# Router logits from 32x32 squares of x turned by VectorE, in a gated cross-attention kernel

## The chip, the cores and the metric

The kernel runs on one core of one Trainium2 chip, in f32. The metric is the device time of one execution in microseconds. Times before are the median of three runs; one further execution was profiled.

## The reference

For a batch of 8, x is 512 x 2048 (features by positions) per batch. Two blocks follow each other: attention within windows of 128 positions, then a router over 64 experts whose tokens are the 512 feature rows.

```python
x = x + jnp.tanh(g_xattn[0]) * xattn(_layernorm(x), ctx, masks, ...)   # D=512, 8 heads of 32, windows of 128
x = x + jnp.tanh(g_ffn[0]) * ffn(_layernorm(x), router_weight, router_bias, expert_bias)

# xattn: q = Wq xn + bq; k = Wk xn + bk; v = Wv ctx + bv        (Wq, Wk, Wv: 256 x 512)
#        attn = softmax(q.T k / sqrt(32), masked); o = gelu(attn v)
#        out = (Wo o + bo) * masks
# ffn:   logits = flat @ router_weight.T + router_bias           (flat: tokens x 2048, 64 experts)
#        w_dense = top-8 of softmax(logits), zero elsewhere; w_sum = their sum
#        out = flat * w_sum + w_dense @ expert_bias
```

The logits sum over the 2048 positions. On the chip x lies with its 512 rows on partitions and the positions along the free axis, so the logits need x turned: positions on the partitions.

## The kernel before

Work is cut into chunks of 512 positions, four per batch, 32 in all, and each chunk into two steps `g`, an even and an odd one, of 256 positions (two windows). Each engine works through its own queue in the order in which the program is written out by hand (`manual_schedule`); SyncE (SP) issues nearly all DMAs from one queue. PSUM has eight banks: `ps_sc` has four (`sc0` to `sc3`, one buffer each), `ps_tr` two (tag `tr`), `ps_mm` two (tag `mm`, taken in turn by `product`).

One step does, in this order:

- `scores(g)`: 16 products for q.T k in 32x128 tiles into the four score banks. `maxima` on VectorE adds the mask and takes row minima, `exps` on ScalarE follows group by group (four groups of four), `divide` is a reciprocal on VectorE and a multiplication on POOL for each half.
- `attend(ch, m)`: the output projection `po` of a finished chunk, 128 rows at a time. VectorE evicts it into `t` (L561), POOL adds it to x in `xr` (L564). Rows 0 and 1 are done in the odd step, in banks `sc1` and `sc2` once the last stage (`steps`) runs, rows 2 and 3 in the next even step, in `mm` banks.
- `queries_and_keys(nxt, e, between)`: q and k of the next chunk, by a scheme of seven block products instead of eight (L356) with sums on VectorE and POOL (L363 to L381). Other work of the step is called from inside it through `between(0)` and `between(1)`.
- `turn_blocks` (L492): VectorE turns the attention weights in 32x32 squares, in two instructions; `move_blocks` (L504): 16 DMAs from SP bring the squares to their places. `weigh` (L523) uses them one step later.
- `values` (L391): v of the next windows, copied out by ScalarE.
- `read_x`: two pieces of a later batch's x (`raw`) get their statistics on VectorE (L251), and SP is told to load the next two.
- `sums_of_x` on POOL and `norm` on ScalarE prepare the chunk after the next.

The second block runs behind. `turn_x(ch, k)` turns one 128-position piece of a finished chunk of x by four TensorE transposes into a `tr` bank (`px`, L579), and ScalarE copies it to `x1T`; there are four such pieces per chunk, all in an even step. `logits(ch)` (L590) in the next odd step multiplies them by the router weights in 64-column halves, right after `exps(g, 1)`; `logits_out` (L606, L608) adds the result to `lgT`. `statistics2` (L574) takes the second layernorm's statistics. When a batch's four chunks are in, the experts are chosen (`gather_halves`, `choose`, `select`, `keep_selected`), and in the eight steps after that `scale_x` on POOL and `mix` (`mixed` L739, `added` L757) finish one eighth of the batch each and store it.

Of the kernel before, what the change touches and what calls it, by code (L numbers as in the profile page):

```python
# [9 lines left out]
F32 = mybir.dt.float32  # L10
# [5 lines left out]
P = 128  # L16
# [6 lines left out]
def flamingo_gated_kernel(  # L23
# [49 lines left out]
    small = ctx.enter_context(tc.tile_pool(name="small", bufs=2))  # L73
    ps_sc = ctx.enter_context(tc.tile_pool(name="ps_sc", bufs=1, space=PSUM))
# [48 lines left out]
    rw_sb = const.tile([P, NK, E], F32, name="rw_sb")  # L123
    eb_sb = const.tile([2 * E, S], F32, name="eb_sb")
# [49 lines left out]
    def load_experts():  # L174
        for i in range(2):
            nc.sync.dma_start(eb_sb[i * E : (i + 1) * E, :], eb)
# [121 lines left out]
    def mask(ch):  # L298

        biases[ch] = work.tile([P, CW], F32, tag="bias", name=f"bias_{ch}")  # L300
        nc.vector.tensor_scalar(biases[ch], mks[ch], 0.0, NEG, ALU.is_le, ALU.mult)
# [39 lines left out]
    def queries_and_keys(ch, e, between):  # L341
# [21 lines left out]
        nc.vector.tensor_copy(s1, p1)  # L363
        nc.vector.tensor_tensor(u2, p6, s1, ALU.add)  # L364
        banks.append(product([P, 2, CW // 2], f"qk_{ch}_{e}_1"))
# [3 lines left out]
        nc.vector.tensor_copy(s5, p5)  # L369
        nc.gpsimd.tensor_tensor(u4, u2, s5, ALU.add)  # L370
        between(0)
        banks.append(product([P, 2, CW // 2], f"qk_{ch}_{e}_2"))
# [5 lines left out]
        between(1)  # L378
        banks.append(product([P, 2, CW // 2], f"qk_{ch}_{e}_3"))
        p4 = block(6, w22, t_[:, 2, :, :])  # L380
        nc.vector.tensor_tensor(q[:, c1], p4, u3, ALU.add)  # L381

    pvs = {}

    def values(ch, h, i, r=None):

        if (ch, h) not in pvs:
            pvs[ch, h] = product([P, NPP, DK], f"pv_{ch}_{h}", r)
# [153 lines left out]
    x1T, lgT, pos, pls = {}, {}, {}, {}  # L542
# [8 lines left out]
    def attend(ch, m, cs=whole, r=None, engine=None, tag=("x1T", 4)):  # L551
# [24 lines left out]
    def turn_x(ch, k, engine=nc.scalar):  # L576
        px = ps_tr.tile([P, NM, P], F32, tag="tr", name=f"px_{ch}_{k}")
        for m in range(NM):
            nc.tensor.transpose(px[:, m, :], xr[ch][:, m, k * P : (k + 1) * P], ident)  # L579
        t = work.tile([P, NM, P], F32, tag="x1T", name=f"x1T_{ch}_{k}", bufs=4)  # L580
        copy(engine, t, px)
        x1T[ch, k] = t

    def logits(ch, ms=slice(0, NM)):


        pl = product([P, D], f"pl_{ch}_{ms.start}")
        for k in range(KC):
            rows = slice((k % 2) * E, (k % 2 + 1) * E)
            nc.tensor.matmul(  # L590
                pl[rows, ms.start * P : ms.stop * P], rw_sb[:, (ch % NCH) * KC + k, :],
                x1T[ch, k][:, ms, :].rearrange("p m d -> p (m d)"),
                start=(k < 2), stop=(k >= KC - 2),
            )
        if ms.stop == NM:
            for k in range(KC):
                del x1T[ch, k]
        pls[ch] = pl

    def logits_out(ch, ms=slice(0, NM)):  # L600
        b = ch // NCH
        ds = slice(ms.start * P, ms.stop * P)
        pl = pls.pop(ch)[:, ds]
        if ch % NCH == 0:
            lgT[b] = work.tile([P, D], F32, tag="lgT", name=f"lgT_{b}", bufs=1)
            nc.vector.tensor_copy(lgT[b], pl)  # L606
        else:
            nc.vector.tensor_tensor(lgT[b][:, ds], pl, lgT[b][:, ds], ALU.add)  # L608
# [123 lines left out]
    def mixed(b, k, stop=True):  # L732
# [3 lines left out]
        for i in range(2):  # L736
# [3 lines left out]
                pt, experts[b]["wT"][rows, mp, :], eb_sb[rows, j * CW : (j + 1) * CW],  # L740
# [111 lines left out]
    for g in range(NG - NH):  # L852
# [20 lines left out]
        def turn_x_(k):  # L873
            if xch is not None:
                turn_x(xch, k)


# [6 lines left out]

        scores(g)
        maxima(g, (0, 1))
# [8 lines left out]

        exps(g, 0)
        exps(g, 1)
        if even and xch is not None:
            attend(xch, 2)
        if lch is not None:  # L900
            logits(lch)
            logits_out(lch)
        maxima(g, (2, 3))
        if even:
            if xch is not None:
# [4 lines left out]
        exps(g, 2)  # L910
# [331 lines left out]
```

## Time and profile before

| | before |
|---|---|
| median of 3 runs | 1237.62 us (1237.52 to 1242.6) |
| profiled execution, its own time | 1242.64 us |
| its span | 1240.9 us |
| granted TensorE clock, mean | 0.996 |
| busy: TensorE, VectorE, ScalarE, POOL | 97%, 78%, 64%, 64% |
| DMA, all queues | 236 MB, mean 190 GB/s |

A row of a group in the profile reads: line, engine, operation, output from input, shapes, count, then busy time in us, the mean of one in ns, and the idle time just before these instructions with what ended it. PE is TensorE, DVE VectorE, ACT ScalarE, SPq the DMA issuing queue of SyncE. A step lasts about 18.3 us, so a chunk about 36.6. Durations of one instruction overlap the next one's start on VectorE and ScalarE, so occupancy is read from start to start.

### The profile page before, as it was taken

To read this page: it belongs to the slowest core of one execution; us is meant where nothing else is said; L and a number is where in the kernel's file an instruction comes from. 1 tells how busy PE (TensorE), PEld (TensorE's weight loads), DVE (VectorE), ACT (ScalarE), POOL (GpSimd) and SP (SyncE) were. 2 spreads that over 40 slices of the span, in tenths; PEclk is the share of its full clock that TensorE was granted. 3 is DMA by queue.
4 is the path that set the end of the run, shared out by engine and by line. 5 is a ranking of instruction groups with operands and counts; after the bars stand their busy time and mean duration, and the time that the engine had idled before them with its cause. 6 is when DMAs were issued, how large, how long until landed. Compare 5 with 4: busy or idle time off the path is not lost.

```text
span 1240.9 us, 27273 instructions
## 1 busy us (share of the span) xinstructions
PE 1209.3 (97%) x8572; PEld 840.5 (68%) x8572; DVE 968.7 (78%) x3549; ACT 795.8 (64%) x2717; POOL 792.5 (64%) x817
## 2 busy tenths in 40 slices
PE   8899989999999999999999999999999999999997
PEld 5766767777677677676677667667667667667553
DVE  5677757888778878888878887788877887778776
ACT  2766646767566657657657566667656757656663
POOL 3654655666577665678566677565667666578544
PEclk9999989999999999999999999999999999999999
DMA  8346655666776676676776676676676766565434
GB/s 288 91 133 178 167 166 134 188 194 190 209 232 196 196 223 185 204 225 183 219 224 190 195 228 198 199 221 182 204 230 199 210 188 193 152 196 160 137 121 184
DMA packets 157280, 236.22 MB, mean 190 GB/s; under 512 B 26192, under 2 KB 60496, under 8 KB 157008
## 3 DMA queue, kind: packets, MB, share of 16 engines
q1 hardware_dynamic: 154816, 231.60, 63.5%
q10 hardware_dynamic: 2320, 2.88, 0.7%
q8 instruction: 68, 1.11, 0.4%
q14 instruction: 76, 0.62, 0.2%
HBM read 137.93 MB, written 33.55 MB: 138 GB/s over the span
## 4 chain that ended last, share of the span: by engine, by line
PE 79%; DVE 8%; DMA 5%; ACT 3%; POOL 2%; issue 2%; SPq 1%; DVEq 0%; ACTq 0%; POOLq 0%
PE qk L356 25%; PE po L555 16%; PE pv L391 16%; PE pa L523 5%; PE sc L419 5%; PE pb L739 4%; PE px L579 4%; PE pl L590 3%; DVE at L442 3%; ACT at L454 2%; DMA raw<-in_x 2%; DMA xr<-in_x 1%; SPq L504 1%; DMA mk<-in_mask_Bx1x_ff 1%; DVE st L251 1%
## 5 line engine op out<-in xcount | busy, mean ns | idle before, releaser
L454 ACT ACTIVATE at<-at,nmx 128x128 f32<-128x128 f32 x1024 | 395.1, 388 | 211.6 <-DVE nmx L442 198.2
L463 POOL TENSOR_TENSOR at<-at,rsum 128x1024 f32<-128x1024 f32 x128 | 242.6, 1895 | 263.1 <-DVE rsum L462 263.1
L391 PE MATMUL pv<-wv_sb,cx 128*128 128x256 f32 x1024 | 250.2, 388 | 2.1 <-DMA cx<-in_ctx 2.1
L555 PE MATMUL po<-o,wo_sb 128*128 128x512 f32 x512 | 234.0, 599 | 0.0
L442 DVE CUSTOM_DVE_ANT_0 at<-sc,bias 128x128 f32<-128x128 f32 x1024 | 224.8, 285 | 10.1 <-PE sc L419 10.1
L564 POOL TENSOR_TENSOR xr<-t,xr 128x512 f32<-128x512 f32 x124 | 156.2, 1272 | 101.2 <-DVE t L561 101.0
L391 PEld LDWEIGHTS pv<-wv_sb,cx 128*128 128x128 f32 x1024 | 187.9, 191 | 38.3 <-issue 12.1
L454 ACT ACTIVATION_READ_ACCUMULATOR at<-at,nmx 128x1 f32 x1024 | 191.8, 187 | 0.0
L492 DVE STREAM_TRANSPOSE blocks<-at 128x1024 f32<-128x1024 f32 x120 | 148.0, 1234 | 23.0 <-DMA atT<-blocks 13.3
L555 PEld LDWEIGHTS po<-o,wo_sb 128*128 128x128 f32 x512 | 94.5, 190 | 97.8 <-issue 83.0
L356 PE MATMUL qk<-xt,wq_sb 128*128 128x256 f32 x496 | 128.7, 382 | 6.7 <-DVE qs L364 6.7
L397 ACT COPY x1T<-px 128x512 f32<-128x512 f32 x120 | 69.0, 583 | 99.2 <-PE px L579 98.1
L356 PE MATMUL qk<-xn,wk_sb 128*128 128x256 f32 x496 | 131.4, 387 | 0.5 <-DVE lgT L606 0.3
L356 PE MATMUL qk<-xn,ws 128*128 128x256 f32 x496 | 127.3, 379 | 0.0
L356 PEld LDWEIGHTS qk<-xn,wk_sb 128*128 128x128 f32 x496 | 89.0, 189 | 51.5 <-DVE nmx L442 29.4
L561 DVE SCALAR_TENSOR_TENSOR t<-po,bo_sb,mk 128x512 f32<-128x512 f32 x128 | 94.8, 746 | 34.8 <-PE po L555 34.5
L356 PEld LDWEIGHTS qk<-xt,wq_sb 128*128 128x128 f32 x496 | 89.3, 190 | 22.4 <-DVE qs L364 10.1
L757 DVE TENSOR_TENSOR xr<-pb,xr 128x512 f32<-128x512 f32 x122 | 78.1, 684 | 33.1 <-PE pb L739 32.5
L356 PEld LDWEIGHTS qk<-xn,ws 128*128 128x128 f32 x496 | 94.2, 190 | 12.8
L251 DVE BATCH_NORM_STATS2 st<-raw 128x6 f32<-128x512 f32 x112 | 72.3, 677 | 34.7 <-DMA raw<-in_x 34.4
L419 PEld LDWEIGHTS sc<-ks,qs 32*128 32x128 f32 x2048 | 65.0, 186 | 47.7 <-issue 22.9
L728 POOL TENSOR_SCALAR xr<-xr,xa,xd 128x512 f32<-128x512 f32 x120 | 92.5, 780 | 0.9
(123 smaller groups left out, 1845.6 us busy)
## 6 DMA issues: line engine op xcount, KB each, us to landing
atT<-blocks SPq DMA_DIRECT2D x960, 64.0 KB, 2.5
out_dram<-xr SPq DMA_DIRECT2D x63, 512.0 KB, 5.9
cx<-in_ctx SPq DMA_DIRECT2D x61, 512.0 KB, 7.6
raw<-in_x SPq DMA_DIRECT2D x112, 256.0 KB, 4.9
xn<-in_x SPq DMA_DIRECT2D x112, 256.0 KB, 3.6
xr<-in_x SPq DMA_DIRECT2D x28, 1024.0 KB, 6.1
mk<-in_mask_Bx1x_ff SPq DMA_DIRECT2D x32, 256.0 KB, 7.2
xr<-in_x SPq DMA_DIRECT2D x12, 256.0 KB, 6.7
```

What stands on the lines that cost most here:

```text
L251: nc.vector.bn_stats(st1[b][:, m, piece, :], x_)
L356: nc.tensor.matmul(out_, w_[:, j, es], xb[:, j, :], start=(j == 0), stop=(j == NM // 2 - 1))
L391: nc.tensor.matmul(pv[:, i, :], cx[:, m, i * W : (i + 1) * W], wv_sb[:, m, :], start=(m == 0), stop=(m == NM - 1),)
L419: nc.tensor.matmul(sc[r][:, i, e, :], qss[ch][rows[r], e, ws], kss[ch][rows[r], e, ws], start=True, stop=True,)
L442: nc.vector.tensor_tensor_reduce(p["at"][i][:, e * HR + r, :], p["sc"][r][:, i, e, :], bias, -scale, BIG, ALU.add, ALU.min, p["nmx"][:, r, ...
L454: nc.scalar.activation(at, at, AF.Exp, bias=p["nmx"][:, r, i, e : e + 1], scale=-1.0, accum_out=p["rsum"][:, i, h : h + 1],)
L463: (engine or nc.gpsimd).tensor_tensor(p["at"][i], p["at"][i], rs[:, :, None].to_broadcast([P, H, W]), ALU.mult)
L492: nc.vector.transpose(p["blocks"][:, :, i, :, :].rearrange("p b h j -> p h b j"), p["at"][i].rearrange("p h (b j) -> p h b j", j=Q),)
L555: nc.tensor.matmul(po[:, cs], wo_sb[:, e, m * P : (m + 1) * P], os_[ch][:, e, cs], start=(e == 0), stop=(e == NE - 1),)
L561: nc.vector.scalar_tensor_tensor(t[:, cs], po[:, cs], bo_sb[:, m : m + 1], mks[ch][:, cs], ALU.add, ALU.mult)
L564: (engine or nc.gpsimd).tensor_tensor(xc, t[:, cs], xc, ALU.add)
L728: nc.gpsimd.tensor_scalar(xc, xc, a, d, ALU.mult, ALU.add)
```

## The change

The logits no longer use x turned by TensorE. VectorE turns x in squares of 32x32 (`turn_x(ch, ms)`, one instruction of 128x512 for each 128 rows), two in the even and two in the odd step, each followed by `statistics2`. A square keeps its 32 rows' partition strip, so `logits` becomes 64 products of 32 positions by 64 experts by 128 rows in 32x64 tiles, into the four score banks, and the router weights are needed in each strip. They are spread once through DRAM (`spread_router`) and loaded for each chunk (`load_router`, 512 KB, from SP in even steps). To make room, the expert biases are loaded again in quarters (`load_experts(j)`), the mask bias has one buffer, and `t` three.

The order changes as well. `queries_and_keys` becomes a generator: its first two pairs of blocks now stand between the exps, its third bank is a `tr` one, and two of its copies go from VectorE to ScalarE. `logits` moves from behind `exps(g, 1)` to behind the first half of `values`, which takes a `tr` bank in odd steps. Choosing the experts moves accordingly.

```diff
-    def load_experts():
+    def load_experts(j):
+        t = work.tile([2 * E, CW], F32, tag="eb", name="eb")
         for i in range(2):
-            nc.sync.dma_start(eb_sb[i * E : (i + 1) * E, :], eb)
+            nc.sync.dma_start(t[i * E : (i + 1) * E, :], eb[:, j * CW : (j + 1) * CW])
+        ebs[j] = t
...
+    def load_router(ch, tag="rw"):
+        t = work.tile([P, NQ, KC, E], F32, tag=tag, name=f"rw_{ch}", bufs=1)
+        nc.sync.dma_start(
+            t.rearrange("p a k e -> p (a k e)"),
+            rw_four[ch % NCH, :, :, :].rearrange("r s f -> (r s) f"),
+        )
+        rws[ch] = t
...
-    def queries_and_keys(ch, e, between):
+    def queries_and_keys(ch, e):
...
-        nc.vector.tensor_copy(s1, p1)
+        nc.scalar.copy(s1, p1)
         nc.vector.tensor_tensor(u2, p6, s1, ALU.add)
+        yield
...
-        nc.vector.tensor_copy(s5, p5)
+        nc.scalar.copy(s5, p5)
         nc.gpsimd.tensor_tensor(u4, u2, s5, ALU.add)
-        between(0)
-        banks.append(product([P, 2, CW // 2], f"qk_{ch}_{e}_2"))
+        yield
+        banks.append(ps_tr.tile([P, 2, CW // 2], F32, tag="tr", name=f"qk_{ch}_{e}_2"))
...
-    def turn_x(ch, k, engine=nc.scalar):
-        px = ps_tr.tile([P, NM, P], F32, tag="tr", name=f"px_{ch}_{k}")
-        for m in range(NM):
-            nc.tensor.transpose(px[:, m, :], xr[ch][:, m, k * P : (k + 1) * P], ident)
-        t = work.tile([P, NM, P], F32, tag="x1T", name=f"x1T_{ch}_{k}", bufs=4)
-        copy(engine, t, px)
-        x1T[ch, k] = t
+    def turn_x(ch, ms, tag="x1b"):
...
+        for m in ms:
+            nc.vector.transpose(
+                x1b[ch][:, :, m, :], xr[ch][:, m, :].rearrange("p (b j) -> p b j", j=Q)
+            )
...
-        pl = product([P, D], f"pl_{ch}_{ms.start}")
-        for k in range(KC):
-            rows = slice((k % 2) * E, (k % 2 + 1) * E)
...
+            pl = [
+                ps_sc.tile([P, n, Q], F32, tag=f"sc{a}", name=f"pl_{ch}_{a}") for a in range(NQ)
+            ]
+        for s_ in range(NB):
+            half_ = slice((s_ % 2) * E, (s_ % 2 + 1) * E)
+            for a in range(NQ):
+                rows = slice(a * Q, (a + 1) * Q)
+                nc.tensor.matmul(
+                    pl[a][half_, :, :].rearrange("p m d -> p (m d)"),
+                    rws[ch][rows, s_ % NQ, s_ // NQ, :],
+                    x1b[ch][rows, s_, ms, :].rearrange("p m d -> p (m d)"),
+                    start=(s_ < 2), stop=(s_ >= NB - 2),
+                )
...
+        for a, pt in enumerate(pls.pop(ch)):
+            t = whole_[:, ms, a, :]
...
+                nc.vector.tensor_tensor(t, pt, t, ALU.add)
...
+        if steps and mk % 2 == 0:
+            load_experts(mk // 2)
+
         scores(g)
-        maxima(g, (0, 1))
+        maxima(g, (0, 1) if even else (0, 1, 2))
...
+        products = queries_and_keys(nxt, h)
         exps(g, 0)
...
+            next(products)
+            exps(g, 2)
+            next(products)
+        else:
+            next(products)
+            maxima(g, (3,))
+            exps(g, 1)
+            next(products)
+            exps(g, 2)
         exps(g, 3)
...
+                if ch >= 2:
+                    ms = (0, 1) if even else (2, 3)
+                    turn_x(ch - 2, ms)
+                    for m in ms:
+                        statistics2(ch - 2, m)
...
-        queries_and_keys(nxt, h, between)
+        between(0)
+        next(products)
+        between(1)
...
+        if xch is not None:
+            load_router(xch)
...
+        if g == 1 or g > 4:
+            read_x(PER)
...
-                values(c_, h_, 0, 0 if g > 1 else None)
+                values(c_, h_, 0, "tr" if g > 1 else None)
+            if lch is not None:
+                logits(lch)
+                logits_out(lch)
             weigh_between()
```

In the new odd step VectorE's queue therefore reads: maxima, evictions of the first two block pairs, the mask, the second reciprocal, `turn_x`, `statistics2`, evictions of the last blocks, `turn_blocks` twice, `read_x`, `logits_out`, the evictions of `po`, the additions of `mix`.

## The prediction

> **What bounds the kernel now.** First the page's busy shares and its chain by engine:
>
> ```profile
> PE 1209.3 (97%) x8572; PEld 840.5 (68%) x8572; DVE 968.7 (78%) x3549; ACT 795.8 (64%) x2717; POOL 792.5 (64%) x817
> ...
> PE 79%; DVE 8%; DMA 5%; ACT 3%; POOL 2%; issue 2%; SPq 1%; DVEq 0%; ACTq 0%; POOLq 0%
> ```
>
> PE is the bound, nearly without holes. Next the chain in order of time, for one even step (from 612.5 us) and the start of the odd one; each row is start, us, matmuls:
>
> ```profile
> 612.58 1.10 PE sc L419 x32
> 613.69 3.63 PE po L555 x8
> 617.32 5.20 PE qk L356 x24
> 622.51 0.44 PE px L579 x4
> ...
> 626.42 1.01 PE pa L523 x32
> ...
> 631.95 1.87 PE pl L590 x8
> 633.82 6.24 PE qk L356 x28
> ```
>
> The next even step's scores start at 649.14 in the timeline, so a pair of steps (one chunk) takes 36.63 us. Every f32 product shows as two records. Then VectorE and the DMA queue of SyncE in that pair, since the change puts work on both:
>
> ```profile
> 625.53 1.23 DVE L492 STREAM_TRANSPOSE blocks<-at 128x1024 f32<-128x1024 f32 x1
> 626.69 2.43 DVE L574 BATCH_NORM_STATS2 st<-xr 128x6 f32<-128x512 f32 x4
> ...
> 645.51 1.39 DVE L251 BATCH_NORM_STATS2 st<-raw 128x6 f32<-128x512 f32 x2 [2.13 <-DMA raw<-in_x]
> ```
>
> ```profile
> 626.80 11.32 SPq L504 DMA_DIRECT2D atT<-blocks  x16
> 638.16 0.58 SPq L115 DMA_DIRECT2D xr<-in_x  x1
> 638.84 0.95 SPq L92 DMA_DIRECT2D raw<-in_x  x2
> ```
>
> See how they hang together: the 16 block moves start when VectorE's second block transpose ends (626.8), take SP 11.32 us, and the raw loads queue behind them. So the odd step's statistics wait for a load that lands 6.7 us after its issue at 638.84. Today that wait of 2.13 us hurts nobody, because PE needs nothing from VectorE until `po`'s evictions.
>
> **PE's saving.** Per chunk, 16 transposes go (0.44 us per four: 1.75) and the old `pl` (1.87): 3.62. What comes is 64 products in 32x64 tiles, 128 records of 128 columns. No row shows that tile. Bounds: `pa` runs 32 such records on four tiles in 1.01 us; if eight tiles go no faster, 128 take 4.05; if eight overlap as four do, 2.0. I take 2.0: `pl`'s two column halves already overlap fully (8 records of 512 columns in 1.87 against 3.63 for `po`'s 8) and `sc`'s four row groups nearly so (1.10). Net 1.6 us per chunk, 31 chunks: 50 us, while PE stays the bound. At the other end, 4.05, PE loses 0.4 per chunk.
> [...]
>
> **The other engines per pair.** VectorE loses four 256-wide copies (24.5+25.7 us over 31 pairs: 1.6), gains four transposes of 128x512 (half of 1.16 start to start is 0.58, the row itself 0.7 with a fixed part; I take 0.63: 2.5) and four logits additions for one (between a quarter of 0.69 and the 256-wide 0.42; I take 0.25: +0.3): net +1.2. At 78% it has room on average. ScalarE trades four 128x512 copies (583 ns) for four of 256 (between the 352 ns of a 128-wide one and 583; 0.35 of occupancy). SP gains three issues, some 1.5 us. The single bias buffer and three `t` buffers cost nothing: VectorE rewrites the mask after its own maxima, and POOL's adds (1.27 each) end long before the third next `attend`; without that cover, one add per pair. On averages all fits; the question is the order.
>
> **Where the order puts it: the even step.** Zero is its first score. Engines work through their queues in order; the trace shows that order as written. PE: scores to 1.1, two `po` to 4.65, first qk pair to 6.4, second to 8.1; results are seen 0.17 later (6.54, 8.28). ScalarE starts the exps at 1.76, one each 0.385: eight are done at 4.85. Now it has a copy of `p1` in its queue, and behind it the rest of the exps: it waits to 6.57, copies to 6.9, four exps to 8.45, copies `p5` to 8.8, last four exps to 10.5. Before, these ended near 8.0. VectorE's second reciprocal waits for that, so 10.6; behind it, two new transposes and two statistics (1.25+1.2) to 13.15; then the evictions of `p7` and `p3` to 13.95. `q[:, c1]` waits for POOL, whose order is now u4 (to 9.6), two divisions (1.85 each, to 13.3), q (to 14.4): 14.8. Two block transposes to 17.2. Before it was 14.25: the block moves start 3.0 us later.
> SP then: 16 issues at 0.63 (today 11.32, with some waits for earlier DMAs that are older by then) 10.1, `xr` 0.63, the new router load 0.63: raw is issued at 28.65. Landing: 6.7 as today plus 0.7 for 512 KB more ahead in the rings (1.34 at 390 GB/s, less the later issue): first raw 36.05, second 36.7. With today's waits and no relief it would be 37.3.
> PE itself ends the even step at 16.45 (18.27 less 1.75, and a little for the order).
>
> **The odd step.** Here `logits` takes all four score banks, after the first half of the values. VectorE's queue reads: ..., block transposes, raw statistics, logits additions. And `attend(pch, 0)` writes bank sc1, so PE cannot start it before the second logits addition, which stands behind the raw statistics, which wait for raw. That is the new wait: statistics end at 37.35, two additions 37.85, `po` 3.55 to 41.4, `pb` 1.06 to **42.45**, the next pair's scores. The loop closes on itself, because these scores start the next exps. Against 36.63: **+5.8 us a pair**. PE's own work in the odd step ends at about 33.8 (it also waits for `pa`'s bank, held by `p7` and `p3`, and for the moved blocks, to 30.9), so some 4 us of PE idle stand before `po`, and both the 1.6 saved and the rate of the 32x64 tiles lie hidden in that hole.
>
> **The sum.** Raw is read with `pb` in the steps between 242 and 1002 us, 20.5 pairs: 119 us. In the six pairs where the experts are selected, selection and match_replace (3.5 us by their rows) stand before the block transposes, against 0.7 that those pairs cost extra today: +2.8 each, some 15 in all with slack. Three earlier pairs have no `pb` and their `po` is in other banks; the scores wait for the last logits addition at 38.4, against 34.9: 11. In four late pairs no raw is read; rival 2's walk below holds without the raw statistics (1.2 less in each step: 37.6): 4. The start (eight DMAs spread the router weights once, 0.6 us of SP each) and the tail, where PE loses transposes and VectorE gains them: zero, within 5 us. Sum 149. The profiled execution took 1242.64 (span 1240.9), 5.0 above the median of three runs; 1237.6 + 149 = 1387.
>
> **A rule against the change: the clock.** This trace has one hole of that size:
>
> ```profile
> 163.01 1.94 PE L523 MATMUL pa<-atT,vT 128*32 128x128 f32 x32 [4.83 <-DMA atT<-blocks]
> ```
>
> ```profile
> 160.00:164.00 4.00, 0.99 (x20) 1.02 (x24) 1.00 (x1) 0.00 (x0) 3.57 (x3) 0.70 0.56 126
> 164.00:168.00 4.00, 4.00 (x27) 3.02 (x20) 2.96 (x5) 0.58 (x1) 0.00 (x0) 0.50 0.74 235
> ```
>
> After 4.83 us idle the granted clock (the column before the last two) is 0.50, and `pa` takes 1.94 instead of 1.08. The clock came back about 5.4 us after PE resumed, so 2.7 us were lost. Holes of 4 us once a pair may or may not cost that: 0 to 2.7 a pair, 0 to 55 in all. I take 0 and keep 55 for the range.
> [...]
>
> **Rivals.**
> 1. PE stays the bound and the 50 us arrive: 1188. For: 97% PE, 62 to 78% elsewhere. Against: the loop above. PE would be ready for that `po` at 30.3 us of the pair (16.45 + 13.9) and gets the addition at 37.85; as raw lands after 33 even in today's trace, it holds only if the raw load gets to SP before the block moves, or the statistics are not ahead of the additions. 0.13.
> 2. Raw comes in time, but VectorE's chain stays: in the odd step exps end at 10.6 after its scores, and reciprocal, transposes, statistics, evictions, blocks, raw statistics and two additions take 8.4 to 19.0; `po` and `pb` give 23.65, a pair of 40.1: 1237.6 + 20.5 x 3.5 + 30 = 1339. 0.20.
> 3. Nothing measurable: gain and waits cancel, or part of the change has no effect. Needs pairs within 0.2 us of today's. 0.03.
> 4. The loop, with the clock halved in every hole: 1442. 0.06.
> My forecast, the raw loop: 0.58.
>
> **Range and chances.** 1262 is rival 2 with three quarters of its cost lost in slack; 1445 takes in the halved clock. Left out are rival 1 and 3 and a few hundredths above. A measurement can tell about 0.5% from no change; faster by more than that is rival 1 (0.13), within it rival 3 (0.03), slower the rest (0.84).
>
> **What would show it.** Right: PE's busy share falls to 80 to 85%; the chain has DMA raw and SP in every pair; `po` waits on VectorE's logits addition for about 4 us in odd steps; the last exp of an even step starts some 2 us later after the scores; the block moves start near 17; VectorE's wait on raw is above the 34.4 us of today. Wrong: PE stays above 95%, a pair takes 35 us, and raw's wait is no longer than today. Then the order on VectorE or SP was misread. That 128 records of `pl` take 2.0 and not 4.05 us can be read from the timeline in any case.

## The result and the profile after

The changed kernel takes 1609.09 us, the median of four runs (1603.76 to 1612.73), beside 1237.74 (1237.52 to 1242.60) for four runs of the kernel before on the same chip. The ratio is 1.2985, with a 95% interval of 1.2931 to 1.3039. The forecast was 1387, with a range up to 1445: slower was right, the size was not.

The page of the profiled execution (1612.73 us, span 1610.9): busy shares and the chain by engine.

```profile
PE 1259.5 (78%) x12020; PEld 907.9 (56%) x12020; DVE 994.5 (62%) x3648; ACT 779.0 (48%) x2717; POOL 792.4 (49%) x817
...
PE 39%; SPq 19%; DMA 15%; DVE 11%; POOL 7%; issue 5%; ACT 3%; DVEq 0%; POOLq 0%; ACTq 0%
```

The span grew by 370.0 us. PE's idle time grew from 31.6 (1240.9 - 1209.3) to 351.4 us, by 319.8; its busy time grew by 50.2, although the change takes some 50 us of work from it. So about 100 us of busy time come from a lower clock, on average 0.885 where it was 0.996: the granted clock is at 0.5 for 370 us, and PE is busy in 216 of them. PE's share of the chain fell from 79% to 39%; SP and DMA now hold a third. The waits of PE say for whom (total us, times, longest):

```profile
PE pl L640 <- DMA rw<-rw_four: 202.7, 29, 9.3
PE pw L764 <- DVE rest L749: 41.1, 7, 5.9
PE qk L391 <- DVE xr L809: 24.8, 18, 1.9
PE qk L391 <- DVE qs L399: 22.4, 1, 22.4
PE pl L640 <- issue: 10.5, 4, 4.5
...
PE pa L562 <- issue: 7.5, 6, 1.8
```

The largest one is a load that is new: the quarter of the router's weights for the very products that wait. One pair of steps in the timeline shows how it comes about. Its even step starts at 792.71 with the scores. First PE in the odd step and at the next pair's start, then SP, then VectorE:

```profile
809.23 1.17 PE L458 MATMUL sc<-ks,qs 32*128 32x128 f32 x32
812.29 1.13 PE L391 MATMUL qk<-xn,wk_sb 128*128 128x256 f32 x4 [1.89 <-DVE xr L809]
...
827.87 3.68 PE L640 MATMUL pl<-x1b,rw 32*64 32x128 f32 x128 [7.54 <-DMA rw<-rw_four]
...
835.10 0.81 PE L430 MATMUL pv<-wv_sb,cx 128*128 128x256 f32 x3 [1.26 <-issue]
835.74 3.60 PE L594 MATMUL po<-o,wo_sb 128*128 128x512 f32 x8
...
840.33 1.17 PE L458 MATMUL sc<-ks,qs 32*128 32x128 f32 x32
```

```profile
810.50 10.26 SPq L543 DMA_DIRECT2D atT<-blocks  x16
...
821.44 0.53 SPq L207 DMA_DIRECT2D rw<-rw_four  x1
822.06 1.06 SPq L93 DMA_DIRECT2D raw<-in_x  x2
```

```profile
829.39 1.33 DVE L286 BATCH_NORM_STATS2 st<-raw 128x6 f32<-128x512 f32 x2 [2.29 <-DMA raw<-in_x]
831.61 0.89 DVE L660 TENSOR_TENSOR lgT<-pl,lgT 128x128 f32<-128x128 f32 x4 [0.89 <-PE pl L640]
```

The router load is issued 28.7 us after the even step's scores, behind 16 block moves, and its products wait for it until 35.16. Raw lands shortly after it; VectorE waits for raw too, but its logits additions then wait for PE (0.89), so raw holds nobody here. The pair takes 47.62 us instead of 36.63. By stretches of the program, from scores to scores:

| us | before | after | forecast of the difference | measured |
|---|---|---|---|---|
| first scores to step 6 | 96.5 | 140.2 | 0 | +43.7 |
| steps 6 to 12 | 112.6 | 129.1 | +11 | +16.5 |
| steps 12 to 62 | 923.1 | 1222.9 | +138 | +299.8 |
| the remainder | 108.6 | 118.7 | 0 | +10.1 |

### The profile page after: what moved, and what is told of

The parts are those of the page before. It is cut to its first block, busy times and chain, and to the rows that moved or that the text cites. A ratio compares the mean times of both kernels' runs of the same rounds, so it can differ in the third digit from the quotient of the medians.

```text
span 1610.9 us, 34491 instructions
## 1 busy us (share of the span) xinstructions
PE 1259.5 (78%) x12020; PEld 907.9 (56%) x12020; DVE 994.5 (62%) x3648; ACT 779.0 (48%) x2717; POOL 792.4 (49%) x817
## 3 DMA queue, kind: packets, MB, share of 16 engines
q8 instruction: 95, 1.56, 0.4%
## 4 chain that ended last, share of the span: by engine, by line
PE 39%; SPq 19%; DMA 15%; DVE 11%; POOL 7%; issue 5%; ACT 3%; DVEq 0%; POOLq 0%; ACTq 0%
SPq L543 17%; PE po L594 13%; DMA rw<-rw_four 11%; PE qk L391 7%; PE pl L640 6%; PE pv L430 5%; POOL at L502 4%; DVE blocks L531 3%; PE pa L562 3%; ACT at L493 2%; PE sc L458 2%; PE pb L791 2%; DMA raw<-in_x 1%; POOL qs L412 1%; DMA mk<-in_mask_Bx1x_ff 1%
## 5 line engine op out<-in xcount | busy, mean ns | idle before, releaser
L640 PE MATMUL pl<-x1b,rw 32*64 32x128 f32 (+1 forms) x4224 | 117.2, 401 | 218.7 <-DMA rw<-rw_four 202.7
L430 PE MATMUL pv<-wv_sb,cx 128*128 128x256 f32 x1024 | 265.0, 404 | 2.9 <-DMA cx<-in_ctx 1.6
L640 PEld LDWEIGHTS pl<-x1b,rw 32*64 32x64 f32 x4224 | 105.9, 206 | 232.5 <-issue 143.5
L430 PEld LDWEIGHTS pv<-wv_sb,cx 128*128 128x128 f32 x1024 | 200.6, 202 | 47.3 <-issue 16.4
L406 POOL TENSOR_TENSOR ks<-qs,s 128x256 f32<-128x256 f32 x62 | 46.2, 744 | 365.3 <-ACT s L405 365.3
L391 PE MATMUL qk<-xt,wq_sb 128*128 128x256 f32 x496 | 132.2, 390 | 29.2 <-DVE qs L399 22.4
L436 ACT COPY o<-pa 128x512 f32<-128x512 f32 x63 | 36.9, 586 | 240.7 <-PE pa L562 239.8
L531 DVE STREAM_TRANSPOSE blocks<-at 128x1024 f32<-128x1024 f32 x120 | 142.3, 1224 | 2.3 <-issue 1.5
L391 PEld LDWEIGHTS qk<-xt,wq_sb 128*128 128x128 f32 x496 | 96.7, 196 | 43.7 <-DVE qs L399 22.8
L501 DVE RECIPROCAL rsum<-rsum 128x8 f32<-128x8 f32 x128 | 25.3, 198 | 153.6 <-ACT at L493 153.6
L809 DVE TENSOR_TENSOR xr<-pb,xr 128x512 f32<-128x512 f32 x122 | 77.9, 682 | 47.7 <-PE pb L791 47.6
```

The costliest lines, as they stand in the source:

```text
L391: nc.tensor.matmul(out_, w_[:, j, es], xb[:, j, :], start=(j == 0), stop=(j == NM // 2 - 1))
L430: nc.tensor.matmul(pv[:, i, :], cx[:, m, i * W : (i + 1) * W], wv_sb[:, m, :], start=(m == 0), stop=(m == NM - 1),)
L531: nc.vector.transpose(p["blocks"][:, :, i, :, :].rearrange("p b h j -> p h b j"), p["at"][i].rearrange("p h (b j) -> p h b j", j=Q),)
L640: nc.tensor.matmul(pl[a][half_, :, :].rearrange("p m d -> p (m d)"), rws[ch][rows, s_ % NQ, s_ // NQ, :], x1b[ch][rows, s_, ms, :].rearran ...
L809: nc.vector.tensor_tensor(xc, pt, xc, ALU.add)
```

## Experiments

Each kernel ran beside the kernel before on the same chip, one execution each where no range is given. The executions of the kernel before lay between 1236.3 and 1244.2, so differences of some 6 us between single runs are not read. "Pair" is the mean of the 20 pairs in steps 12 to 52; 37.1 us before, 48.2 after. The theory in the beginning: the router load is the new wait, and behind it stand others of the same kind. The rivals: the halved clock, and the small products themselves.

**1. The router load moved.**

```diff
+        if xch is not None:
+            load_router(xch)         # head of the even step, ahead of scores(g)
...
-        if xch is not None:
-            load_router(xch)         # behind move_blocks
```

> The changed kernel, with the one load of the router weights issued at the head of the even step, ahead of the 16 block moves, instead of behind them. Theory A (TensorE's logits wait for this load because SP issues it behind the moves; the loop of 47.6 us a pair runs through it): the wait of pl on the router load (202.7 us) all but vanishes, and the next latest arrival takes over, the raw statistics ahead of the logits additions: pairs of 41 to 43 us, 1400 to 1460 us in all. Theory B (VectorE's order alone sets the pair, the load is only the last of several): a pair loses under 2 us, above 1550 us. Theory C (26 MB more DMA traffic slows every load): no change, 1600 us.

Measured: 1539.9 us, pair 46.6, clock 0.924. Between the expectations. The 203 us of wait are gone, 69 us of time. Others stepped in, so its total was not its price:

```profile
PE pl L640 <- DVE x1b L622: 53.2, 31, 4.7
...
PE po L594 <- DVE lgT L660: 28.9, 8, 4.9
```

The second of these waits is the one that was forecast. The shortest of the 20 pairs of this run, whose even step starts at 336.23, shows it bare; SP, VectorE and PE:

```profile
365.17 0.95 SPq L93 DMA_DIRECT2D raw<-in_x  x2
```

```profile
372.68 0.69 DVE L286 BATCH_NORM_STATS2 st<-raw 128x6 f32<-128x512 f32 x1 [0.16 <-DMA raw<-in_x]
373.29 0.87 DVE L660 TENSOR_TENSOR lgT<-pl,lgT 128x128 f32<-128x128 f32 x4
```

```profile
373.91 3.67 PE L594 MATMUL po<-o,wo_sb 128*128 128x512 f32 x8 [3.64 <-DVE lgT L660]
```

Counted from the even step's scores, raw is issued at 28.94 (28.65 in the forecast), its statistics end at 37.14 (37.35), `po` starts at 37.68 (37.85), and the pair takes 42.34 us (42.45).

**2. The hole filled, to keep the clock.**

```diff
+            for _ in range(28):      # ahead of the products of pl, into its bank
+                nc.tensor.matmul(pl[0]..., ones, ones, start=True, stop=True)
```

> The changed kernel, with 28 idle-time products of 128x128 (ones by ones, into the first logits bank before it is started) ahead of the 64 logits products, so that TensorE has about 6.3 us of work in its hole of 7.5. Theory A with the clock as a second part: the granted clock rises from 0.885 to above 0.96, pl takes 1.9 instead of 3.7 us and the products behind it run at full rate, some 3 us less per pair: 1500 to 1540 us. If the halved clock costs nothing because everything behind it waits anyway: 1600 us. If the filled time itself is on the path: above 1650 us.

Measured: 1624.6 us, pair 48.9, clock 0.942. The wait for the router load falls from 203 to 47 us, by 156, but the filling products themselves take 192, so they overrun the hole by some 36 us; the 64 logits products take 83 us in all instead of 117. What the clock gives back is about what the filling costs, so this run gives no price for the clock. As the first cause it falls: its whole lengthening of PE's busy time is about 100 of the 371 us.

**3. Raw statistics behind the logits additions, on top of 1.**

```diff
-        if g == 1 or g > 4:
+        if g == 1 or g > 4 and lch is None:
             read_x(PER)
...
                 logits_out(lch)
+                read_x(PER)
```

> As the run with the router load first, and in odd steps the raw statistics stand behind the logits additions in VectorE's queue. Theory A with raw next (the loop that was forecast): pairs fall to about 39, where VectorE's chain (second reciprocal, squares, statistics, evictions, blocks, additions) sets them: 1330 to 1380 us. If raw was not the next wait, the time equals that of the run with the router load first.

Measured: 1509.1, pair 45.2. A gain of 31 us, far less than expected. The largest wait is still that of `pl` for the squares (`x1b`), 50.7 us; and now `pb` waits 28.7 us for the expert bias, whose quarters are issued in the step that uses them.

**4. VectorE's and PE's order mended further, on top of 3.**

```diff
+                if ch >= 2:
+                    turn_x(ch - 2, (0, 1) if even else (2, 3))   # ahead of the second reciprocal
                 divide(g, 1)
...
+        if lch is not None:                                      # ahead of between(1)
+            values(nxt, h, 0, "tr"); logits(lch); logits_out(lch)
```

> As the run before, and VectorE's queue is reordered: the squares of x are turned ahead of the second reciprocal (in its wait for the exps), statistics2 stands behind the block transposes, and in odd steps the logits and their additions stand ahead of the block transposes. Theory B as the second layer (VectorE's order is what is left): the hole before po closes, pairs of 36.5 to 37.5, 1270 to 1310 us with a start some 40 us longer than before. If something else holds the odd step (the shared banks, POOL, DMA), the time stays within 20 us of the run before.

Measured: 1499.2, pair 44.5; a miss by 190. `pb`'s wait for the expert bias rose to 47.6 us. Mending one wait after another did not lead back, so the next runs cut the change in two instead.

**5. The order alone, without squares.** The kernel before, with the generator, the copies on ScalarE and the third bank from `tr`; x turned by TensorE as before.

```diff
-        queries_and_keys(nxt, h, between)
+        products = queries_and_keys(nxt, h)   # two pieces between the exps
...
+        between(0)
+        next(products)
+        between(1)
```

> The kernel before, with one part of the change alone: the products of the queries and keys are written in three pieces between the exponentials, p1 and p5 leave by ScalarE, the third bank is taken from the turning banks. x is still transposed by TensorE and weighted in four 64-column products. Theory A (the time goes in the order of the small work on VectorE, ScalarE and SP, and the squares by themselves are cheap): the exponentials end some 2.5 us later in each step, with everything behind them, and a pair grows by 2 to 5 us: 1280 to 1340. Theory B (the squares themselves bring the loss, by their instruction fetches, their router load and the clock that halves behind them): within 10 us of 1238.

Measured: 1373.0, pair 41.9, clock 0.979. The order alone costs 134 us, more than expected.

**6. The squares alone, in the order of before.**

```diff
+        if even and g + NH >= LAG:
+            load_experts((g + NH - LAG) % SPB // 2)    # a pair ahead
+        if xch is not None and g > 4:
+            load_router(xch)                           # four loads of 32 partitions from rw_once
...
         queries_and_keys(nxt, h, between)              # as in the kernel before
+        if lch is not None:
+            logits(lch)
...
             move_blocks(g, loads)
+        if lch is not None:
+            logits_out(lch)
+        if xch is not None:
+            turn_x(xch, range(NM))                     # all four squares, then the statistics
```

> The other half of the change alone, with its own order mended: the products of queries and keys, their copies on VectorE and the exponentials stand as in the kernel before; the four squares of a chunk are all turned at the end of the even step behind the block moves, the statistics stay where they were; the 64 small products come right behind the queries and keys of the odd step, their additions behind its block moves and ahead of its raw statistics; the router's quarter is loaded at the head of the even step, by four loads of 32 partitions from one copy in DRAM (no fourfold copy at the start); the expert bias is loaded one pair of steps ahead. Theory A: TensorE stays the bound, a pair is 36.7 minus 1.6 plus up to 1 for fetches: 1195 to 1245, granted clock 0.98 and over. Theory B: the small products still cost fetch stalls of 2 to 4 us a pair and some of the clock: 1290 to 1350.

Measured: 1382.6, pair 40.8, clock 0.953: 143 us. So each half costs about as much as the forecast gave to the whole. In the timeline, PE at the head of an odd step (scores at 686.53), and VectorE before it:

```profile
690.85 2.06 PE L387 MATMUL qk<-xn,wk_sb 128*128 128x256 f32 x4 [3.14 <-DVE xr L804]
692.70 1.83 PE L387 MATMUL qk<-xt,ws 128*128 128x256 f32 x4
```

```profile
684.21 2.45 DVE L617 STREAM_TRANSPOSE x1b<-xr 128x512 f32<-128x512 f32 x4
686.58 2.43 DVE L608 BATCH_NORM_STATS2 st<-xr 128x6 f32<-128x512 f32 x4
688.93 1.27 DVE L282 BATCH_NORM_STATS2 st<-raw 128x6 f32<-128x512 f32 x2
690.12 1.27 DVE L804 TENSOR_TENSOR xr<-pb,xr 128x512 f32<-128x512 f32 x2
```

The first product needs the bank that the mix addition frees. TensorE is there 1.8 us earlier than before (even steps of 16.5 instead of 18.27), VectorE 2.45 later. The hole is followed by half-speed products (4 in 2.06 and 1.83 instead of 1.03; the granted clock is 0.51 from 691.00 to 694.40).

**7. The start.** The changed kernel without the four copies of 512 KB in DRAM.

```diff
-        for r in range(NQ):
-            nc.sync.dma_start(rw_four[:, r, :, :], rw_once...)
...
+        for r in range(NQ):                    # load_router: four loads from rw_once
+            nc.sync.dma_start(t[r * Q : (r + 1) * Q, ...], rw_once[ch % NCH, ...])
```

> The changed kernel, but the router's quarter comes by four loads of 32 partitions each from the one copy in DRAM; the four copies of 512 KB from DRAM to DRAM at the start are gone. If those copies hold the loads of raw back in steps 4 and 5 (a step of 51 us where the one before took 20), the stretch from the first scores to step 6 falls from 140 to 100 to 112 us and the kernel to 1570 to 1585; the three more issues on SP (0.6 us each) may take 1 us of each pair back. If the start is late for another reason it stays at 135 to 145.

Measured: 1601.8; the stretch to step 6 falls from 140.2 to 116.6, but the pair rises to 49.1, so that the kernel as a whole gains only 7 us. The copies held SP's raw loads, and these everything behind them; the changed kernel's row, 3.7 us after the first copy's issue:

```profile
125.54 23.00 SPq L93 DMA_DIRECT2D raw<-in_x  x4
```

Without them the same raw row takes 6.76. That is 24 of the 44 us that the start had grown by.

**8. What in the order costs: the copies.** Kernel 5 with `p1` and `p5` (two of the seven block products) copied by VectorE again.

```diff
-        nc.scalar.copy(s1, p1)
+        nc.vector.tensor_copy(s1, p1)
```

> f2_order_alone with the copies of p1 and p5 back on VectorE; the products still stand between the exponentials in the program, which leaves ScalarE's queue nothing to wait for. Theory A (the copies on ScalarE, which wait 3.1 and 0.4 us for TensorE in the middle of the exponentials, are what the order costs): 1236 to 1260. Theory B (it is the bank from the turning banks, or VectorE's order): 1330 to 1375.

Measured: 1354.2, pair 41.1. The copies on ScalarE are only 19 of the 134 us. Theory A of that run falls. The timeline, VectorE and then PE:

```profile
685.96 0.42 DVE L381 TENSOR_TENSOR qs<-qk,qs 128x256 f32<-128x256 f32 x1 [3.44 <-POOL qs L377]
686.33 2.37 DVE L493 STREAM_TRANSPOSE blocks<-at 128x1024 f32<-128x1024 f32 x2
```

```profile
692.89 1.94 PE L591 MATMUL pl<-x1T,rw_sb 128*64 128x512 f32 x8 [1.39 <-DVE xr L758]
```

The last eviction (`p4`) waits 3.44 us for POOL, which divides twice first, and both block transposes stand behind it, and behind these the statistics and the mix addition, for which the next step's logits wait 1.39. In the kernel before one transpose stood ahead of that eviction and filled the wait.

**9. One block transpose ahead of the last eviction again, on top of 8.**

```diff
         nc.vector.scalar_tensor_tensor(k[:, c2], p3, bk_, u4, ALU.add, ALU.add)
+        yield                                   # between(1) runs here
```

> f7_order_copies_on_vector with the first block transpose ahead of the last eviction of the queries (p4 + u3), as in the kernel before. In f7 that eviction waits 3.4 us in each step for GpSimd, which is at its second normalisation, and both block transposes wait behind it. Theory A (this place alone is the 115 us): 1236 to 1250. Theory B (the products between the exponentials, or the third bank from the turning banks, cost time by themselves): over 1300.

Measured: 1280.6, pair 38.2, clock 0.991. One place in VectorE's queue is worth 74 us; 41 us stay with the products between the exponentials and the third bank from `tr`, which no run separates, 12 of them before step 6.

**10. Only the squares' time on VectorE.** The kernel before, nothing taken away, four idle transposes a pair (and the mask's single buffer, to make room for their target).

```diff
+        if xch is not None:
+            for m in range(NM):
+                nc.vector.transpose(idle..., xr[xch][:, m, :]...)
```

> The kernel before, with nothing taken away, and four more 32x32 transposes of 128x512 on VectorE in each even step behind the block moves, into a tile that nobody reads (x is still transposed by TensorE): 2.45 us of VectorE's time a pair, without the squares' products, loads or banks. Theory A (VectorE had no room for them there): the mix additions come 2.45 us later and a pair grows by 2 to 5 us: 1290 to 1360. Theory B (VectorE, busy 74% of the time, had room): 1240 to 1255.

Measured: 1292.0, pair 39.2: 54 us for 2.45 us of VectorE in 29 pairs (71 us of work). VectorE had almost no room there; no wait for the mask shows in this trace. PE's new wait is the mix addition:

```profile
PE pl L591 <- DVE xr L758: 37.7, 24, 2.4
```

**11. Kernel 6 with the statistics of x1 moved to the odd step.**

```diff
         if lch is not None:
             logits_out(lch)
+            for m in range(NM):
+                statistics2(lch, m)
```

> f3_squares_in_old_order with VectorE's even step unloaded: the four statistics of x1 (2.4 us) go to the odd step, behind the additions of the logits, where VectorE waited 2.9 us for raw; the raw statistics go ahead of the squares. Theory A (TensorE is no longer the bound: VectorE's step is longer than TensorE's, so its mix additions come late and hold the first products of queries and keys of the odd step): the wait for the mix additions (62 us) falls by more than half, the odd step from 23.6 to 19 to 21, the kernel to 1250 to 1300. Theory B (the odd step is long because of the small products): 1370 to 1390.

Measured: 1394.5, pair 41.8. The wait for the mix additions fell from 62 to 19 us as expected, but scores now wait 26 us for evictions of `po` by VectorE, and the pairs that select experts got longer (up to 52.6 us instead of 43.3). Moving work within VectorE's queue did not help.

**12. Work taken off VectorE.** Kernel 6 with all statistics over 64 of 512 columns, which leaves part of them out.

```diff
-        nc.vector.bn_stats(st1[b][:, m, piece, :], x_)
+        nc.vector.bn_stats(st1[b][:, m, piece, :], x_[:, 0:64])
```

> f3_squares_in_old_order with all statistics taken over 64 of 512 columns (part of the computation left out), which takes some 4 us of VectorE's time out of each pair; everything else, the small products, their loads and banks, is as it was. Theory A (VectorE had no room for the squares; TensorE's saving then shows): the odd step falls from 23.6 to 18.5 to 19.5, a pair is 35 to 36, the kernel 1190 to 1225. Theory B (the small products, the router's loads or the clock behind them cost it): 1340 to 1380.

Measured: 1360.9, pair 41.1: only 22 us, nearly all outside these pairs. Theory A's number is missed; the time is in B's range, and of B's candidates the timeline names the loads. SP, VectorE and PE in one odd step:

```profile
672.27 0.42 SPq L105 DMA_DIRECT2D cx<-in_ctx  x1
672.78 2.19 SPq L182 DMA_DIRECT2D eb<-in_L_ffn_expert_bias  x2
675.03 1.98 SPq L203 DMA_DIRECT2D rw<-rw_once  x4
677.95 0.36 SPq L110 DMA_DIRECT2D mk<-in_mask_Bx1x_ff  x1
681.03 10.63 SPq L538 DMA_DIRECT2D atT<-blocks  x16
```

```profile
693.31 1.25 DVE L526 STREAM_TRANSPOSE blocks<-at 128x1024 f32<-128x1024 f32 x1 [6.50 <-DMA atT<-blocks]
```

```profile
693.33 1.37 PE L557 MATMUL pa<-atT,vT 128*32 128x128 f32 x32 [2.73 <-DMA atT<-blocks]
```

VectorE was done with the block transposes at 674.96, yet the moves start 6 us later. SP is at the new loads ahead of them until 678.31, and then waits 2.7 us for the landing of `cx`, issued ahead of two `eb`, four `rw` and `mk`. So the blocks' single buffer comes free late, and VectorE's transposes and `pa` wait.

**13. VectorE's room given by other means, everything computed.** Kernel 11 with raw's statistics as two sums on ScalarE from batch 2 on.

```diff
+            for k, f in enumerate((AF.Identity, AF.Square)):
+                nc.scalar.activation(t, t, f, accum_out=st1[b][:, k, m, j : j + 1])
```

> f5_statistics_moved, with the statistics of the next batches' x (raw) taken by ScalarE from batch 2 on, as two sums with accumulators at the end of each step, where it waited 3.6 to 4.6 us for the maxima; the statistics of the last chunk of a batch stay in the even step; the whole expert bias is loaded one step earlier. That takes 2.5 us a pair from VectorE and gives 5 to 6 us to ScalarE. Theory A (VectorE's room is the limit): 1200 to 1270. If ScalarE becomes late instead (its sums wait for raw and hold the next exponentials): 1300 to 1400.

Measured: 1353.28 (1351.83 to 1353.83), ratio 1.0919 (1.0887 to 1.0951), pair 40.6. The same limit as in 12: VectorE waits 104 us for the block moves.

**14 to 16. The six loads issued by ScalarE**, at the end of the odd step: on kernel 6, on 12, on 13. Before the last steps, the whole expert bias is loaded earlier too.

```diff
+        if not even and 5 <= g < NG - NH - 1:
+            load_router(ch - 1, queue=nc.scalar)
+            if g + 1 >= LAG:
+                load_experts((g + 1 - LAG) % SPB // 2, nc.scalar)
```

> f3_squares_in_old_order with the router's four loads and the expert bias's two issued by ScalarE's queue at the end of the odd step before, instead of SP's queue at the head of the even step. Theory A (both VectorE's room and SP's queue limit the squares): the moves' wait for ctx (85 us) falls under 30, the kernel 1310 to 1360. Theory B (SP's queue alone): 1200 to 1250. Theory C (neither, the products): 1375 to 1390.

> g2_room_on_vector (statistics over 64 of 512 columns: part of the computation left out) with the same six loads off SP. Theory A and B: with both limits away TensorE is the bound again, a pair is 35.1 to 36.5, the kernel 1195 to 1240, granted clock 0.985 and over. Theory C: over 1330.

> g3_statistics_on_scalar (everything computed, the next batches' statistics on ScalarE) with the same six loads off SP. Theory A: 1215 to 1275. If ScalarE's sums and issues make the exponentials late: 1290 to 1350. Theory C: 1345 to 1360.

Measured: 1440.9, 1415.4 and 1492.2, pairs of 44.1, 43.7 and 46.3: all worse, by 58, 55 and 139. In the second the wait of VectorE for the moves is no longer among its longest and the odd step takes 21.3 us on average instead of 24.0; but the even step takes 22.4 instead of 17.1, since ScalarE now stands at its own issues, with the next exponentials behind:

```profile
684.73 5.42 ACTq L203 DMA_DIRECT2D rw<-rw_once  x4
```

**17 and 18. Fewer issues ahead of the moves**, on 12 and on 13: the router's quarter in one load from the fourfold copy, the expert bias behind the moves.

```diff
-        if even and g + NH >= LAG:
-            load_experts((g + NH - LAG) % SPB // 2)
...
             load_xr(ch - 1)
+        if even and LAG <= g + NH < NG - NH:
+            load_experts((g + NH - LAG) % SPB // 2)
```

> g2_room_on_vector (statistics over 64 of 512 columns: part of the computation left out), with the router's quarter in one load from the fourfold copy (which costs some 24 us at the start) at the head of the even step, and the expert bias loaded behind the block moves of the even step, a pair ahead. Theory A (place and number of the loads ahead of the moves): the moves' wait for ctx falls from 93 to under 30 us, VectorE's wait for the moves from 118 to under 30, an odd step is 20 to 21 and a pair 36.5 to 38, about the pair of the kernel before, since 2 us of the odd step's wait for VectorE's evictions stay: 1255 to 1300. Theory B (it was something else): 1340 to 1380.

> g3_statistics_on_scalar (everything computed) with the same loads. Theory A: 1260 to 1310, still not below the kernel before. Theory B: 1340 to 1380.

Measured: 1327.2 (pair 38.9) and 1340.43 (1339.31 to 1344.90, ratio 1.0823, 1.0797 to 1.0849; pair 38.8). Theory A's pair is there: in the first of these, a plain pair from 657.07 to 694.38 takes 37.31. VectorE's wait for the moves fell from 118 to 47 us, SP's for `cx` from 93 to 53 us (so not under 30). The totals were missed, by the start (+28) and by the pairs that select experts. What stays in the plain odd step, at 673.58:

```profile
675.10 1.13 PE L391 MATMUL qk<-xn,wk_sb 128*128 128x256 f32 x4 [0.34 <-DVE xr L809]
...
680.16 1.13 PE L391 MATMUL qk<-xt,wq_sb 128*128 128x256 f32 x4 [1.34 <-DVE qs L399]
```

Both are VectorE's: the mix addition, then `u2`, which stands behind all sixteen maxima. In the kernel before, the old `pl` (1.9 us) stood between the scores and these products and covered that time. The new products need the four score banks, so they cannot stand there. In this pair the odd step loses 2.4 us and the even step gains 1.8, so 37.3 is no better than the 36.63 of before.

## Why the prediction was wrong

**PE's saving: right.** The even step was walked to 16.45 us and takes 16.52 (792.71 to 809.23), 18.27 before. The 128 records of `pl` were put at 2.0 of 2.0 to 4.05; they take 2.10 (run 6; run 12 at a granted clock of 1.00) and 2.15 (run 17). The work is saved; nothing of it arrives as time.

**The even step's walk: right.** Exponentials end 10.8 us after the scores (10.5 forecast), the block transposes at 17.8 (17.2), the moves take 10.26 (10.1), raw is issued at 29.35 (28.65).

**The odd step: here it failed.** The forecast counted the router load as an issue on SP (0.63) and as 512 KB ahead of raw, and never asked who waits for it. The next product of the logits does. By the forecast's own walk the load was issued near 28.0, after moves and `xr`; with a landing of some 6 us (the median in the changed kernel is 6.3) `pl` could start at about 34, and `pa`, the values, `po` and `pb` still follow. Instead the text placed `pl` before 33.8 and hid it in the hole in front of `po`. In the pair shown `pl` starts at 35.16, takes 3.6 at half clock, `pa` and the values 4.3 with a stop of 1.26; `po` starts at 43.03, where the forecast had 37.85. That is the difference of 5.2 us between a pair of 47.62 and the forecast 42.45.

The load explains less than half of this by itself. The 15 pairs of steps 12 to 52 that select no experts take 47.36 us on average, 4.9 more than forecast. `pl` starts at 34.9 in them; with `pl` at full clock (2.1) and what follows without stops (7.4, as in three of these pairs) they would take 44.5, which is 2.0 over the forecast. The half clock in `pl` (3.8 on average) adds 1.7, half clock and stops between `pl` and `po` add 1.2. So the wait that was left out makes the hole, and the zero that was taken for the clock more than doubles its price.

**The wait that was forecast** (raw, its statistics, the additions, `po`) is real and of the size forecast, but it lies under the other one. In the changed kernel no `po` waits for the additions; once the router load is moved, one pair of run 1 follows the forecast's walk to within 0.3 us, and takes 42.34. The other plain pairs of that run are longer: on average `po` and `pb` take 5.9 us instead of 4.6, in part at half clock behind the hole, and PE stops for 2.7 to 5.0 us in five of the 20. Moving raw's statistics brings 31 us (run 3). The mechanism was one of several of a size, not the one that set the end.

**"On averages all fits" was true and misled.** VectorE's +1.2 us a pair were counted at nothing. Run 10 shows that 2.45 us at that place cost 54 us of time by themselves; runs 11 and 12 that taking them elsewhere or away uncovers the next limit, the block moves on SP behind six more loads.

**The order's price** was put into the walk as 3 us later moves, without effect on PE but through raw. Alone it costs 134 us (run 5): 19 are the copies (8), 74 one transpose behind an eviction that waits for POOL (9), and 41 stay. In the timeline of run 8 the mix additions end up behind the next scores, and the next products wait for them.

**The sum of the parts.** Order alone 134, squares alone 143, the router load's place 69 (run 1), the copies at the start 24 (run 7): 370, beside 371 measured. That is no proof. The first two are measured in the kernel before and the last two within the changed kernel, 24 is one stretch of a run that gained 7 us as a whole, and the 69 contain a part of the clock's price. The closeness is luck in part.

**Smaller terms.** Pairs that select experts: right. They take 50.6 us on average against 47.4 for the others (3.2 more), and took 37.6 against 36.9 in the kernel before (0.7 more); the forecast had +2.8 each, 2.5 came, with `pw` waiting up to 5.9 for the selection. Start: "zero, within 5" became 43.7; the 2 MB copied in DRAM were counted as issues and not as transfers in front of raw, which is 24 of it (run 7), and the rest was not taken apart. Tail: 10.

**The clock.** Zero was taken, up to 55 us kept. On the way to the next scores the half clock costs the 15 plain pairs about 2.3 us each (1.7 in `pl`, 0.6 behind it), close to the 2.7 a pair that were kept for the range. It also stood behind holes smaller than the one of 4.83 us in the trace of before: 3.14 us in run 6 (granted clock 0.51 behind it), 2.73 in run 12 (0.50 from 694 to 697). In run 1, where the first product of an odd step waited 1.91 us for VectorE (the clock is the column before the last two):

```profile
771.50:774.90 3.40, 1.49 (x28) 1.19 (x24) 3.40 (x8) 0.00 (x0) 0.00 (x0) 0.98 0.20 48
774.90:778.30 3.40, 3.40 (x10) 2.72 (x9) 2.90 (x26) 2.72 (x14) 0.00 (x0) 0.52 0.44 106
```

PE was busy for 1.49 of 3.4 us, and in the next 3.4 us the granted clock was 0.52. The length of the hole alone did not decide: in the changed kernel the clock was 1.00 from 812.30 to 815.70, behind the hole of 1.89 us (812.29 above), and the four products from 813.26 took 1.03. These cases give no condition for the halving. The zero was taken for holes of 4 us; the router load makes holes of 7.5, and behind the one shown `pl` took 3.68 us at a granted clock of 0.52.

**The rivals.** The first (1188) is refuted in every run: with the known limits cut down the plain pair shown for run 17 still takes 37.3. It has the small products in it, at 2.15 us, so they are not the first cause either. The second (VectorE's chain, pair 40.1) names a true second layer; the pairs of 46.6 and 45.2 in runs 1 and 3 contain other waits besides, so its price alone was not measured. The signs that were named: SP and DMA in the chain were seen, the last exponential came 2.8 us later (2 named), the moves started at 17.8 (17); PE's busy share was 78%, under the 80 to 85 named. VectorE's wait for raw was above 34.4 us (49.8), but 22.3 of it are one wait in the start, so in the pairs it is shorter than before. `po` waiting 4 us for the additions was seen in run 1 only (3.64).

**Open.** What remains of the order's 41 us, and of run 17's 88, was not taken apart, nor what the clock would be worth by itself. What causes the stops before which the profile shows nothing ("issue", 1.26 above, 18 us at `pl` and `pa`) was not shown: the changed kernel has 12020 records of products instead of 8572, and its instruction queue moved 1.56 MB instead of 1.11, but no run took these away.

## What to carry to other kernels

For every new load ask three things: what is ahead of it in its queue, when it lands, and which instruction of the bound engine needs it; a load counted only by its issue and its bytes is not counted. When the bound engine is made faster, the second engine's order becomes the bound: walk its queue to the point where it frees a bank for the first, since a share of 78% says nothing about room at that place. A wait's total in the profile is an upper limit of its worth (203 us gave 69); where several of a size lie over each other, cut the change in halves before mending them one by one.

## What the runs showed of the hardware

- Four loads issued by ScalarE took 5.42 us in its queue (run 15), with the exponentials behind them; the kernels with such loads were 55 to 139 us slower (runs 14 to 16).
- On SP block moves waited for the landing of `cx`, a load issued before them: 31.9 us in 28 waits in the kernel before, 93.2 in 52 in run 12, 53.2 in 36 in run 17, with fewer loads ahead of the moves. Why a move waits for a load that it does not use was not shown.
- Four copies of 512 KB within DRAM kept four raw loads of 256 KB at the issue for 23.0 us instead of 6.76.
- The granted clock of TensorE was at half behind some of its holes: 0.52 behind 7.54 us in the changed kernel, 0.51 behind 3.14 (run 6), 0.50 behind 2.73 (run 12), 0.52 behind 1.91 (run 1); behind 1.89 us in the changed kernel it was 1.00. In the changed kernel it was at half for 370 of 1610.9 us.
- 128 records of 128 columns in 32x64 tiles took 2.10 us (runs 6 and 12), 16 ns each; `pa`'s 32 records of 128 columns in 128x32 tiles took 1.08 us in run 6, 34 ns each.
